# Moving one block of row normalisation out of the first up stage into the attention rounds

## The chip, the cores and the metric

The kernel runs on one core of a Trainium2 chip. The metric is device microseconds of one execution; three executions of the kernel before took 2329.0 to 2330.51, median 2329.72. All times below are microseconds (us) unless marked ns.

TensorE (PE) multiplies, with its weight loads (PEld) shown apart; VectorE (DVE) and ScalarE (ACT) work elementwise; GpSimd (POOL) and SyncE (SP) do little here but issue DMAs. Each engine works through its own queue in order.

## The reference

One transformer block, all in 32-bit floats, on an input of 2 x 2048 x 1024: attention on the normalised rows, then a feed-forward part on the normalised result, both with a residual.

```python
q, k, v = split(layernorm(x) @ Wqkv + bqkv)            # each 2048 x 256
x1 = x + softmax(q @ k.T / 16) @ v @ Wo + bo
z = layernorm(x1)
rw = sum of the two largest of z @ gate_w (8 columns)
f = relu(z @ up_w) ** 2 @ down_w + ((z @ fc1_w) @ expert_w * rw) @ fc2_w
out = x1 + layernorm(f) * ln_gamma + ln_beta
```

## The kernel before, in words

Tokens are handled in eight blocks of 512 rows, each of four row tiles of 128 x 1024. Every product is done three times, with numbers split into a high and a low half (`split`, L140: ScalarE casts the high half, L142, VectorE subtracts to get the low one, L143; `split_late` does the same with the subtraction put off, L149 and L150). The matrix products all stand in `Pass3.add` (L130).

**Projection.** First Q, K and V of all blocks are made (to some 300 us); K and V of the second sequence go to memory and come back later.

**Attention rounds** (L792 on, n = 1 to 8). Round n computes the scores of block n and the product with V of block n - 1, side by side. For each of 16 key chunks k, `scores` makes six matmuls into a PSUM bank of the two-bank pool `psb`; ScalarE copies the bank (L626) and VectorE takes the running maximum (L631); then the bank may be written again. `softmax` subtracts the maximum (L666), takes the exponential on ScalarE (L667), splits the result and adds it to the row sum (L675, L678). At the end `row_max` makes the maximum over all keys (L640), `finish` evacuates the product (L697, L698), and `project` (L707 on) multiplies by Wo: for each of the four row tiles SP loads the residual row (`xres`, L712), GpSimd adds bo to it by an accumulating DMA (L713), VectorE scales each of two banks and adds it to that row (L725), and SP stores the row to `x1` (L728). In rounds 2 to 7 at k = 2 and k = 8 GpSimd also issues a sum of weight quarters between DRAM tensors (`sum_step`, L406 and L408), behind the last bo addition.

**First block of the feed-forward part.** Rounds 2 to 5 load a row tile of `x1[0]` at k = 8 (L818); rounds 3 to 6 normalise it at k = 5 (`norm_row`, L820): BATCH_NORM_STATS on VectorE (L178, L180), the root on ScalarE (L182), the normalisation on VectorE (L203), a transposition in 32 x 32 squares (L213), and a store to a DRAM tile `xt_d` (L218). The last round fetches the four tiles back (`fetch_tile`, L226) and splits them.

**Feed-forward part** (L1142 on). Four passes of 1024 rows (two blocks), each with an up stage and a down stage. A scheme with seven products instead of eight quarters is used, so weights and inputs come in sums of quarters. In the first pass, weight pieces are loaded as `raw` (L903) on SP's queue, cast on ScalarE (L929), split on VectorE (L936), and every other piece is stored for later passes by GpSimd (L939). The second block of the first pass (`x1[1]`) is normalised inside this first up stage: `norm2 = Norm(1)` (L1146), and one `norm2.step()` after each of eleven of the first twelve pieces (L1266). A step loads a row on SP's queue (L1044), makes its statistics, normalises another on ScalarE (L285), transposes and stores a third on GpSimd's queue (L1046), and fetches a fourth. Rows 0 and 2 get their statistics from ScalarE (`Moments`: Identity with a running sum, L261; Square, L273; the root, L274), rows 1 and 3 from VectorE (`Stats`). The fetched tiles are used from the eleventh piece on (L1276). For later passes the same is done in the down stage before.

**What sets the order.** The feed-forward part stands under `tc.manual_schedule()`: each engine gets its instructions in the order of the program. The attention rounds do not: a scheduler orders each engine's queue by the program's priorities and its own estimates of time, and hands out the slots of the tile pools. A row tile (pool `row`, 9 slots of 128 x 1024) holds a residual row, a sum, a loaded Q row, a row to be normalised, or its transposed copy; a load waits until its slot is free, and what stands behind it on SP's queue waits with it.

Of the kernel before, what the change touches and what calls it, by code (L numbers as in the profile page):

```python
# [17 lines left out]
P = 128  # L18
# [7 lines left out]
def kernel(  # L26
# [21 lines left out]
    nc = tc.nc  # L48
# [11 lines left out]
    NB = W // P  # L60
# [20 lines left out]
    def unit(name, dtype=FR):  # L81
        return up.tile([P, U], dtype, tag="u", name=name)
# [4 lines left out]
    def row(name):  # L87
        return rp.tile([P, C], FP, tag="r", name=name)
# [21 lines left out]
    x1 = [dram.tile([W, C], FP, name=f"x1_{i}") for i in range(NBLK)]  # L110
# [29 lines left out]
    def split(t, hi, lo, eng=nc.vector):  # L140

        nc.scalar.copy(hi, t)  # L142
        eng.tensor_tensor(lo, t, f32(hi), ALU.subtract)  # L143
# [46 lines left out]
    def load_row(src, q=nc.sync):  # L190
        r = row("xrow")
        q.dma_start(out=r, in_=src)
        return r

    def norm_row(r, q=nc.gpsimd):
        return norm_write(r, row_stats(r), q)

    def row_stats(r):
        return ln_stats([r[:, ts(h, W)] for h in range(C // W)])
# [5 lines left out]
    def norm_write(r, stats, q=nc.gpsimd):  # L205


        normalise(r, stats)
        return transpose_write(r, q)

    def transpose_write(r, q=nc.gpsimd):
        b = row("xblk")
        nc.vector.transpose(  # L213
            b.rearrange("p (q k i) -> p q k i", q=P // SQ, i=SQ),
            r.rearrange("p (k i q) -> p q k i", k=NCC, i=SQ),
        )
        d = dram.tile([P, C], FP, tag="xt", name="xt_d", bufs=8)
        q.dma_start(out=d, in_=b)  # L218
        return d
# [3 lines left out]
    def fetch_tile(d, q=nc.gpsimd):  # L223

        xt = row("xt")
        fetched[0] = q.dma_start(  # L226
            out=xt.rearrange("p (a f) -> p a f", a=P // SQ),
            in_=d.rearrange("(a i) (q f) -> (i q) a f", i=SQ, q=P // SQ),
        )
        return xt  # L230
# [13 lines left out]
    def split_x(xts, half, t, X, split=split):  # L244
        xv = xts[t].rearrange("p (a k j) -> p k a j", k=NCC, j=SQ)[:, ts(half, NCC // 2)]
        hi, lo = (
            v.rearrange("p (c n) -> p c n", n=W)[:, :, ts(t, P)].rearrange(
                "p c (a j) -> p c a j", j=SQ
            )
            for v in X  # L250
        )
        split(xv, hi, lo)
# [342 lines left out]
    def load_kv(name, src, alloc):  # L595
        t = alloc(name)
        nc.sync.dma_start(out=f32(t), in_=src)
        return t
# [4 lines left out]
    def kv_home(j):  # L603
        return ex_unit if j < 2 * BPB - 1 else unit
# [4 lines left out]
    def start(n, r):  # L609
        st[n] = {"s": [], "p": [], "q": split_q(n, r)}  # L610

    def scores(n, k):
        s = st[n]
        if k % 4 == 0:
            s["s"].append(unit(f"s{n}_{k // 4}", FP))

        wide = n == 0 or n == 1 and k < LAG + 2
        pm = bank(psa if wide and k % 3 else psb, "ps")
        acc = Pass3(pm, NDC)
        kk, q = hl(kv_chunk(n, 0, k)), hl(s["q"])  # L620
        for dc in range(NDC):
            acc.add(
                tuple(kk[:, i, ds(dc * W + (k % 4) * P, P)] for i in range(2)),
                tuple(q[:, i, ts(dc, W)] for i in range(2)),
            )
        nc.scalar.copy(s["s"][k // 4][:, ts(k % 4, W)], pm)  # L626
        if k == 0:
            s["max"] = half(f"max{n}")
            nc.scalar.copy(s["max"], pm)  # L629
        else:  # L630
            nc.vector.tensor_tensor(s["max"], pm, s["max"], ALU.max)  # L631
# [48 lines left out]
    def values(n, k):  # L680
        s = st[n]
        if k == 0:
            s["o"] = [Pass3(bank(psa, "po"), NKC) for _ in range(NDC)]
        v = hl(kv_chunk(n, 1, k))
        for dc in range(NDC):
            s["o"][dc].add(
                tuple(v[:, i, ds((k % 4) * D + dc * P, P)] for i in range(2)),
                tuple(hl(s["p"][k // 2])[:, i, ts(k % 2, W)] for i in range(2)),
            )
# [98 lines left out]

    g_f = half("g_f")[:, : NCC * NE].rearrange("p (c e) -> p c e", c=NCC)
    nc.gpsimd.dma_start(out=g_f, in_=gate_w.rearrange("(c p) e -> p c e", p=P))  # L790
    xts = []
    for n in range(1, NBLK + 1):  # L792
        if n == NBLK:
            X = {p: (unit("xh"), unit("xl")) for p in ("p1", "p2")}

        lag = LAG if n > 1 else LAG + 2
        for k in range(NKC + lag):
            if n + 1 < NBLK:
                if k == 0:
                    q_row = load_row(q_d[n + 1])  # L800
                elif k == NKC // 2:
                    start(n + 1, q_row)
            if n < NBLK and k < NKC:
                scores(n, k)
            if k >= lag:
                values(n - 1, k - lag)
                if n == BPB and (k - LAG) % 4 == 3:
                    j = BPB + (k - LAG) // 4
                    kv[j].append(load_kv(f"v{j}", v_d[j], kv_home(j)))
            if n == 1 and k == 1:  # L810
                softmax(0, 0)
            if n == 1 and k % 2 and 1 < k < NKC:
                softmax(0, k // 2)
            elif n > 1 and k % 2 == 0 and k + 2 < NKC:
                softmax(n - 1, k // 2 + 1)

            if k == NKC // 2 and n in range(2, 2 + NB):
                xts.append(load_row(x1[0][ts(n - 2, P), :]))  # L818
            elif k == 5 and n in range(3, 3 + NB):
                xts[n - 3] = norm_row(xts[n - 3], nc.sync)  # L820
            elif n == NBLK:
                if k < NB:
                    xts[k] = fetch_tile(xts[k], nc.sync)
                elif k % 2 == 0 and k >= 6 and k < 6 + 2 * NB:
                    split_x(xts, 0, k // 2 - 3, X["p1"])
            if k in (2, 8) and 1 < n < NBLK:
                with tc.issue_after(last[0].ins):
                    sum_step(steps.pop(0))
            if n == 1 and k == NKC // 2:
                wo = unit("wo_h"), unit("wo_l")  # L830
                for dc in range(NDC):
                    split(wo_f[dc], *(v[:, ts(dc, C)] for v in wo))
                split(g_f, gate[:, :, 0:NE], gate[:, :, NE : 2 * NE])
            if k == NKC - 1:
                if n == BPB - 1:
                    for j in range(BPB, 2 * BPB):
                        kv[j] = [load_kv(f"k{j}", k_d[j], kv_home(j))]
                if n < NBLK:
                    row_max(n)
        finish(n - 1)  # L840
        if n < NBLK:
            softmax(n, 0)
        project(n - 1)
# [184 lines left out]
    class Norm:  # L1028
# [8 lines left out]
        def step(self, halves=(0, 1)):  # L1037

            load, first, second, norm, write, fetch = (
                self.i - lag for lag in (0, 2, 3, 4, 5, 7)  # L1040
            )
            if 0 in halves:
                if load in range(NB):
                    self.r[load] = load_row(x1[self.n][ts(load, P), :])  # L1044
                if write in range(NB):
                    self.d[write] = transpose_write(self.r[write])  # L1046
                if norm in range(NB):
                    self.m[norm].normalise()
            if 1 in halves:
                if second in range(NB):  # L1050
                    self.m[second].second()
                if first in range(NB):

                    r, by_dve = self.r[first], self.n == 1 and first % 2
                    self.m[first] = Stats(r) if by_dve else Moments(r, "n")
                if fetch in range(NB):
                    self.x[fetch] = fetch_tile(self.d[fetch])
                self.i += 1
# [54 lines left out]
    res_pair, todo, loaded, first, second, written = [], [], [], [], [], []  # L1113
# [28 lines left out]
    t1 = xts  # L1142
    with tc.manual_schedule():
        for b in range(NBB):
            if b == 0:
                norm2 = Norm(1)  # L1146
            x_t = [t1, None]

            h = {}
# [67 lines left out]
            for m, (p, i) in enumerate(UPS[b]):  # L1217
# [45 lines left out]

                if m % 2 and m < 17:
                    out_step()
                if b == 0 and m in (0, 1, 2, 3, 4, 6, 7, 8, 9, 10, 11):  # L1266
                    norm2.step()
                if b == 0 and m < NB:
                    split_x(x_t[0], 1, m, X["p2"], split_late)
                if b == 0 and m % 2 == 0 and 24 <= m < 24 + 4 * NK:  # L1270
# [2 lines left out]

                m4 = 10
                if m == m4:
                    x_t[1] = norm2.x  # L1276
                    X["p4"] = new_x()
                if m > m4 and (m - m4) % 2 and (m - m4) // 2 < NB:
                    split_x(x_t[1], 1, (m - m4) // 2, X["p4"], split_late)
                elif m >= 2 * NK and p != "p7":  # L1280
                    n = {"p4": "p6", "p6": "p5", "p5": "p3", "p3": "p7"}[p]
# [40 lines left out]
            if more:  # L1322
                norm1, norm2 = Norm(2 * b + 2), Norm(2 * b + 3)
            for j, p in enumerate(("p1", "p2", "p6", "p5", "p3", "p7", "p4")):
# [12 lines left out]
                for k in range(NK - late):  # L1337
# [4 lines left out]
                    if more:  # L1342
# [3 lines left out]
                        if j >= 5 and k % 2 and k < 2 * NB:  # L1346
                            n = "p1" if j == 5 else "p2"
# [101 lines left out]
```

## Time and profile before

| what | value |
|---|---|
| three runs, median (lowest to highest) | 2329.72 (2329.0 to 2330.51) us |
| the profiled execution, its own time | 2328.82 us |
| its span in the profile | 2327.1 us |
| granted TensorE clock, mean | 0.998 |
| weight loads busy | 82% |
| bytes moved by DMA | 555.19 MB, mean 239 GB/s |
| HBM read and written | 418.55 and 185.60 MB |

The profile's page lists busy times, the span in 40 slices, the DMA queues, the chain of work that ended last, and the costliest groups of instructions by line. Further views of the same trace give the waits (who waited for whom), the instructions in order of time, DMA issues with the time to their landing, and busy times by stretch. A matmul's end is modelled: a row shows 0.39 us for one, though the next begins 0.23 us later, so a short stall can hide under the shown length, and starts are compared here, not lengths.

### The profile page before, as it was taken

To read this page: it belongs to the slowest core of one execution; us is meant where nothing else is said; L and a number is where in the kernel's file an instruction comes from. 1 tells how busy PE (TensorE), PEld (TensorE's weight loads), DVE (VectorE), ACT (ScalarE), POOL (GpSimd) and SP (SyncE) were. 2 spreads that over 40 slices of the span, in tenths; PEclk is the share of its full clock that TensorE was granted. 3 is DMA by queue.
4 is the path that set the end of the run, shared out by engine and by line. 5 is a ranking of instruction groups with operands and counts; after the bars stand their busy time and mean duration, and the time that the engine had idled before them with its cause. 6 is when DMAs were issued, how large, how long until landed. Compare 5 with 4: busy or idle time off the path is not lost.

```text
span 2327.1 us, 28783 instructions
## 1 busy us (share of the span) xinstructions
PE 2311.7 (99%) x10396; PEld 1898.8 (82%) x10396; DVE 1535.6 (66%) x2315; ACT 1174.4 (50%) x1927; POOL 283.8 (12%) x428
## 2 busy tenths in 40 slices
PE   9999999999999999999999999999999999999998
PEld 7888888888888788888788888878888887888886
DVE  6666569888888575797655577754456675435557
ACT  6555455555543633766552474664055556214235
POOL 3222111011000111110110011110000011000000
PEclk9999999999999999999999999999999999999999
DMA  7878659799977877786887688696568579565684
GB/s 258 301 275 276 240 156 256 232 302 293 228 178 226 269 223 234 241 288 196 251 248 252 219 307 307 189 284 219 194 208 273 193 236 329 188 193 182 204 245 151
DMA packets 226046, 555.19 MB, mean 239 GB/s; under 512 B 18369, under 2 KB 89537, under 8 KB 223857
## 3 DMA queue, kind: packets, MB, share of 16 engines
q1 hardware_dynamic: 158928, 310.43, 40.3%
q0 software_dynamic: 66976, 242.94, 35.5%
q8 instruction: 82, 1.34, 0.2%
q14 instruction: 60, 0.48, 0.1%
HBM read 418.55 MB, written 185.60 MB: 260 GB/s over the span
## 4 chain that ended last, share of the span: by engine, by line
PE 96%; DMA 1%; issue 1%; DVE 1%; ACT 1%; POOL 0%; DVEq 0%; SPq 0%; ACTq 0%; POOLq 0%
PE pd L130 32%; PE pu L130 31%; PE pq L130 7%; PE po L130 7%; PE ps L130 7%; PE pv L446 4%; PE pw L130 4%; PE pg L985 1%; PE pf L130 1%; DMA raw<-in_L_ffn_fc_w_dram 0%; DMA xt<-xt_d 0%; PE psum L701 0%; DVE w L936 0%; DMA w_p<-w 0%; PE pmx L638 0%
## 5 line engine op out<-in xcount | busy, mean ns | idle before, releaser
L130 PE MATMUL pd<-w,sp 128*128 128x512 f32 x3336 | 757.9, 389 | 0.1
L130 PEld LDWEIGHTS pd<-w,sp 128*128 128x128 f32 x3336 | 626.2, 188 | 130.7 <-DVE sp L1192 0.5
L130 PE MATMUL pu<-xh,w 128*128 128x512 f32 x2240 | 693.1, 390 | 1.5 <-DVE w L936 1.4
L130 PEld LDWEIGHTS pu<-xh,w 128*128 128x128 f32 x2240 | 419.3, 188 | 91.2 <-DVE w L936 2.6
L130 PE MATMUL pu<-xl,w 128*128 128x512 f32 x1120 | 436.1, 389 | 0.0
L130 PEld LDWEIGHTS pu<-xl,w 128*128 128x128 f32 x1120 | 210.3, 188 | 44.3 <-DVE xl L150 0.3
L1187 ACT CAST sp<-h 128x512 fp32r<-128x512 f32 x238 | 146.5, 619 | 167.6 <-PE pd L130 130.9
L936 DVE TENSOR_TENSOR w<-w 128x512 fp32r<-128x512 f32 x245 | 167.2, 685 | 80.8 <-ACT w L929 76.9
L929 ACT CAST w<-w 128x512 fp32r<-128x512 f32 x245 | 149.5, 616 | 136.8 <-DMA w<-wt 119.5
L1192 DVE TENSOR_TENSOR sp<-h,sp 128x512 fp32r<-128x512 f32 x238 | 162.5, 685 | 65.6 <-ACT sp L1187 65.4
L130 PE MATMUL po<-p,v 128*128 128x512 f32 x768 | 194.3, 391 | 0.6 <-DVE p L143 0.6
L130 PE MATMUL ps<-q,k 128*128 128x512 f32 x768 | 192.4, 390 | 0.0
L130 PEld LDWEIGHTS ps<-q,k 128*128 128x128 f32 x768 | 143.6, 188 | 30.0 <-ACT max L629 0.2
L130 PEld LDWEIGHTS po<-p,v 128*128 128x128 f32 x768 | 143.0, 188 | 30.2 <-DVE p L143 1.0
L150 DVE TENSOR_TENSOR xl<-xt,xh 128x512 fp32r<-128x512 f32 x108 | 74.3, 688 | 129.8 <-ACT xh L149 129.8
L1137 ACT ACTIVATE h<-h 128x1024 f32<-128x1024 f32 x48 | 50.6, 1055 | 207.5 <-DVE h L1247 158.4
L626 ACT COPY s<-ps 128x512 f32<-128x512 f32 x128 | 74.9, 586 | 135.0 <-PE ps L130 134.9
L213 DVE STREAM_TRANSPOSE xblk<-xrow 128x1024 f32<-128x1024 f32 x60 | 120.8, 2014 | 8.7 <-ACT xrow L285 8.7
L939 POOL DMA_DIRECT2D w_p<-w x105 | 56.1, 535 | 463.6 <-DVE w L936 369.5
L631 DVE TENSOR_TENSOR max<-ps,max 128x512 f32<-128x512 f32 x120 | 82.1, 684 | 33.1 <-ACT s L626 32.1
L130 PE MATMUL pq<-xha,w_h 128*128 128x512 f32 x256 | 99.6, 389 | 0.0
L130 PE MATMUL pq<-xha,w_l 128*128 128x512 f32 x256 | 99.6, 389 | 0.0
(198 smaller groups left out, 2995.4 us busy)
## 6 DMA issues: line engine op xcount, KB each, us to landing
w<-w_p SPq DMA_DIRECT2D x260, 512.0 KB, 3.7
w<-wt SPq DMA_DIRECT2D x235, 256.0 KB, 3.4
w_p<-w POOLq DMA_DIRECT2D x105, 512.0 KB, 4.6
xt_d<-xblk POOLq DMA_DIRECT2D x56, 512.0 KB, 4.1
xt<-xt_d POOLq DMA_DIRECT2D x56, 512.0 KB, 5.7
xres<-in_L_attn_x_dram SPq DMA_DIRECT2D x32, 512.0 KB, 6.9
xres<-in_L_attn_bo_dram POOLq DMA_DIRECT2D x32, 512.0 KB, 10.4
x<-xres SPq DMA_DIRECT2D x32, 512.0 KB, 4.5
```

Source lines behind the costliest of these rows:

```text
L130: nc.tensor.matmul(self.ps, lhsT=a, rhs=b, start=self.i == 0, stop=self.i == self.n - 1, skip_group_check=self.on,)
L150: late_ops.append(lambda: nc.vector.tensor_tensor(lo, t, f32(hi), ALU.subtract))
L213: nc.vector.transpose(b.rearrange("p (q k i) -> p q k i", q=P // SQ, i=SQ), r.rearrange("p (k i q) -> p q k i", k=NCC, i=SQ),)
L446: nc.tensor.matmul(o, lhsT=x_, rhs=w_, start=c + i == 0, stop=c == NCC - 1 and i == 1, skip_group_check=True,)
L626: nc.scalar.copy(s["s"][k // 4][:, ts(k % 4, W)], pm)
L631: nc.vector.tensor_tensor(s["max"], pm, s["max"], ALU.max)
L929: nc.scalar.copy(w[:, 0:W], raw)
L936: nc.vector.tensor_tensor(w[:, W : 2 * W], raw, f32(w)[:, 0:W], ALU.subtract)
L939: nc.gpsimd.dma_start(out=kept[key], in_=w.bitcast(FP))
L1137: nc.scalar.activation(o, v, AF.Relu)
L1187: nc.scalar.copy(t[:, 0:W], v)
L1192: add(t[:, W : 2 * W], v, f32(t)[:, 0:W], ALU.subtract)
```

## The change

The four row tiles of `x1[1]` are loaded, normalised, transposed and stored in rounds 3 to 6, one in each, beside the row of `x1[0]` that is already there: load at k = 6, statistics by ScalarE (`Moments`) at k = 10, normalisation at k = 12, transposition and store (now on SP's queue) at k = 14. The first up stage only fetches the four stored tiles, after pieces 1, 3, 5 and 7. `Norm.step` loses its case for VectorE statistics, which only that block used.

```diff
-    xts = []
+    xts, seconds = [], []
...
             elif k == 5 and n in range(3, 3 + NB):
                 xts[n - 3] = norm_row(xts[n - 3], nc.sync)
+            elif k == 6 and n in range(3, 3 + NB):
+                second_row = load_row(x1[1][ts(n - 3, P), :])
+            elif k == 10 and n in range(3, 3 + NB):
+                second_m = Moments(second_row, "n")
+                second_m.second()
+            elif k == 12 and n in range(3, 3 + NB):
+                second_m.normalise()
+            elif k == 14 and n in range(3, 3 + NB):
+                seconds.append(transpose_write(second_row, nc.sync))
             elif n == NBLK:
...
                 if first in range(NB):
-
-                    r, by_dve = self.r[first], self.n == 1 and first % 2
-                    self.m[first] = Stats(r) if by_dve else Moments(r, "n")
+                    self.m[first] = Moments(self.r[first], "n")
...
         for b in range(NBB):
-            if b == 0:
-                norm2 = Norm(1)
             x_t = [t1, None]
...
-                if b == 0 and m in (0, 1, 2, 3, 4, 6, 7, 8, 9, 10, 11):
-                    norm2.step()
+                if b == 0 and m % 2 and m < 2 * NB:
+                    seconds[m // 2] = fetch_tile(seconds[m // 2])
...
                 m4 = 10
                 if m == m4:
-                    x_t[1] = norm2.x
+                    x_t[1] = norm2.x if b else seconds
```

## The prediction

> **What bounds the kernel now.** I read the first page from the top: busy shares, the chain that ended last, then TensorE's waits.
>
> ```profile
> span 2327.1 us, 28783 instructions
> PE 2311.7 (99%) x10396; PEld 1898.8 (82%) x10396; DVE 1535.6 (66%) x2315; ACT 1174.4 (50%) x1927; POOL 283.8 (12%) x428
> PEclk9999999999999999999999999999999999999999
> PE 96%; DMA 1%; issue 1%; DVE 1%; ACT 1%; POOL 0%; DVEq 0%; SPq 0%; ACTq 0%; POOLq 0%
> ```
>
> TensorE is the bound: 99% busy at full clock, and 96% of the chain. The change neither adds nor removes a matmul, and in the built order of the changed kernel TensorE's rows stand as before, one for one. So only TensorE's stalls can change. All those that the trace names are these (columns: who waited for whom, total, times, longest):
>
> ```profile
> PE busy L513 <- POOL ident masks.py:199: 2.7, 1, 2.7
> PE pu L130 <- DVE w L936: 1.4, 1, 1.4
> PE pt L520 <- DMA ew<-in_L_ffn_expert_w_dram: 0.7, 1, 0.7
> PE po L130 <- DVE p L143: 0.6, 1, 0.6
> ```
>
> The first and third lie in the first 5 us, out of reach. The second is in the first up stage. Next I cut the span into stretches. The columns are the stretch, its length, then busy time and instructions of TensorE, weight loads, VectorE, ScalarE and GpSimd, granted clock, DMA share, GB/s: rounds 3, 4 and 5 (from one output projection to the next), two parts of round 3, the first up stage behind the last projection, the second up stage.
>
> ```profile
> 427.87:484.38 56.51, 56.51 (x258) 46.56 (x257) 49.28 (x60) 30.24 (x40) 6.82 (x8) 1.00 0.84 252
> 484.38:540.82 56.44, 56.44 (x258) 46.58 (x257) 49.22 (x60) 30.21 (x40) 6.78 (x8) 1.00 1.02 307
> 540.82:597.27 56.45, 56.45 (x257) 46.56 (x257) 49.20 (x60) 30.23 (x40) 7.99 (x8) 1.00 1.05 271
> 444.00:466.00 22.00, 22.00 (x98) 18.20 (x97) 21.75 (x26) 13.68 (x18) 3.60 (x5) 1.00 1.00 314
> 466.00:486.00 20.00, 20.00 (x96) 16.34 (x95) 13.38 (x19) 12.16 (x17) 3.22 (x4) 1.00 1.05 269
> 754.99:954.74 199.75, 198.28 (x877) 159.30 (x876) 124.79 (x207) 105.75 (x167) 34.10 (x62) 1.00 0.76 240
> 1145.41:1345.52 200.11, 200.11 (x889) 161.88 (x889) 110.07 (x173) 90.71 (x147) 20.73 (x36) 1.00 0.77 245
> ```
>
> The reader is to see three things. TensorE has no idle time in the rounds, so the place that receives the work can gain nothing. VectorE is 87% busy there, and full from 444 to 466 (21.75 of 22), with slack only in the tail of the round. And the up stage that gives the work away runs little longer than an undisturbed one.
>
> **What the up stage can give back.** TensorE did its first group of 12 matmuls before 754.99. At the steady 0.2267 us each (46 projection matmuls took 10.43 us in the chain) that is 2.72, so the stage cost 199.75 + 2.72 = 202.47 us. The second up stage, with the same matmuls, took 200.11. The excess of 2.4 us is all that can be gained. One stall holds most of it: the last matmul before it starts at 806.02, the next at 807.82, where 806.25 was due, so 1.6 us.
>
> ```profile
> 806.02 0.39 PE L130 MATMUL pu<-xh,w 128*128 128x512 f32 x1
> 807.82 0.50 PE L130 MATMUL pu<-xh,w 128*128 128x512 f32 x1 [1.41 <-DVE w L936]
> ```
>
> The chain of waits behind it: the split at 807.08 stood in VectorE's queue behind the split of a fc1_w piece, whose load was issued only at 794.34 and took 9.30 us; its issue waited for a buffer freed behind work that waited 6.93 us for the fetch of a normalised row, issued at 785.38 after that row's transposition. The change takes out of this stage four transpositions (L213, 4 x 2.02), four BATCH_NORM_STATS (2.6), and some 1.9 us of small instructions, 12.6 us of VectorE; on ScalarE four normalisations (5.0), two Identity and two Square passes (4.4), a table load (1.3), four roots and the small rest (2.4), 13.1 us; four row loads from SP's queue, four row stores from GpSimd's. The four fetches stay but come by the eighth piece, long before use. I take 1.6 for the stall and half of the other 0.8: **-2.0 us**, between 0 (the fc1_w load is late by itself) and -2.4.
>
> **What the rounds must take.** Each of rounds 3 to 6 gets one row. VectorE: one transposition (1.99) and two small instructions (0.16 each), 2.3 us: 49.2 becomes 51.5 of 56.45. ScalarE: Identity and Square passes (1.05 and 1.14, with 0.19 each to read the sum), the mean (0.20), the root (0.30), the normalisation (1.24) and two more table loads (1.28 each), 6.9 us: 30.2 becomes 37.1. TensorE waits in a round if a score bank is still unread: scores k+2 need the maximum k (L631) done. I laid the new order of both queues for round 4 over the durations above and round 3's dates. The new statistics come between scores 4 and 8. ScalarE runs the Square until 452.9, copies scores 7, loads a table, takes the root, copies scores 8 (454.9), loads again (to 456.75), then does the exponential (457.75), a cast (458.75) and the copy of scores 9 (459.3). VectorE then goes: maximum 8 to 456.3, subtraction to 457.45, reciprocal, BATCH_NORM_STATS and product to 458.4, sum to 459.5, a low half to 460.65, maximum 9 to 461.25. TensorE wants that bank for scores 11 at 461.48 (scores begin 1.56 before their copy, here 463.04). Before, maximum 9 ended at 459.4. So 2.0 us of slack become 0.2; at the other maxima 1.4 or more remains. The transposition falls behind maximum 11, at 465.4 to 467.3, in the tail. I take 0.1 a round, **+0.4 us**; bounds 0 (TensorE is saturated: no gain) and 4 x 2.3 = 9.2, if every added VectorE microsecond reached TensorE.
>
> The Trainium skill, "ScalarE: Activation LUTs", section "What ACT_TABLE_LOAD costs", prices a switch of table sets at about 2.66 us, the load and as much again for a drain, and its section on table sets advises to do all of one set before the other, which speaks against this change. The trace shows 1283 ns a load and the next ScalarE instruction 1.28 us after the load began (764.94, then 766.24), so no drain. By the page, an estimate: two switches 2.76 us longer would make maximum 9 late and cost some 2.5 us in each of four rounds, 10 us; by the row, nothing.
>
> **The row slots and SP's queue.** Row tiles share 9 slots, and a round now holds two more. In the built order this moves the residual loads (xres, L712): before, all four are issued early (444.7 to 452.5 in round 3, 500.7 to 502.9 in round 4); now only the first stands ahead of the new row's store on SP's queue, the second behind it, and the third and fourth also behind the loads of K (round 3) or V (round 4), which wait for a buffer. That store waits for the transposition, 467.3 in round 3. GpSimd then adds bo by a DMA of its own (L713), and L725 needs the sum. The wait is not in this trace; these are its rows (KB each, median us to landing, both rounds):
>
> ```profile
> xres<-in_L_attn_bo_dram POOLq DMA_DIRECT2D x8, 512.0 KB, 11.3
> ...
> xres<-in_L_attn_x_dram SPq DMA_DIRECT2D x5, 512.0 KB, 6.5
> ```
>
> Round 3: K's buffer frees near 469.5, so row three is issued at 470.0; with 6.5, 0.9 (GpSimd's issue) and 11.3 it is ready at 488.7, due at 490.77: hidden. Round 4: V's last buffer freed at 529.1, so row three goes out at 529.5 and is ready at 548.2, due at 547.20: 1.0 late. Round 5 has no K or V: row two goes out at 580.5 and is ready at 599.2, due at 600.9. VectorE's next maxima wait behind L725, with 0.4 us of slack there (maximum 1 ended at 440.03, scores 3 began at 440.40), so round 4 loses 0.6: I take **+0.7 us** for all. Ends: nothing, with the shortest rows (5.8 and 8.1), and with the longest of both rounds (12.0 and 17.1) 9 to 12 us in each of rounds 3 and 4. Behind the fourth bo the weight sums (L406, L408) start 14 us later in round 3 and some 29 later in round 4; they took 20 to 42 us to land, and the rounds after have room: nothing.
>
> **Sum.** The profiled run took 2328.82 us (span 2327.1 and 1.7 around it). 2328.82 - 2.0 + 0.4 + 0.7 = 2327.9. The median of three is 2329.72, 0.9 above that run, so on its footing **2328.8 us**. A measurement of this kernel tells about 0.2% (4.7 us) from no change; this is well inside.
>
> **Rivals.**
> Late residual rows (slower): the loads and additions of rounds 3 to 6, four where DMA share is already 0.84 to 1.05, take as long as the slower rows here: 9 (between 6.5 and 12.0), 0.9 and 14.5 (between 11.7 and 17.1), 24.4 us. Then row three is late by 3.6 in round 3 and 6.7 in round 4, row two by 4.0 in round 5, and by some 2 in round 6: 16 us, 2345. It decides where issue to readiness exceeds 17.7 us in round 4 and some 20.5 in rounds 3 and 5. For it: the DMA share, and SP's order. Against: the old 17.1 us came fourth of a burst of four additions (9.7, 11.7, 14.0, 17.1), and the new bursts are of two or three. A loss over 0.2% needs 6.7 us of stalls.
> Full queues: VectorE's 2.3 us reach TensorE in part, say 1 us a round: 2328.8 + 3.6 = 2332.4, still inside 0.2%. For it: the full 444 to 466 stretch. Against: the transposition falls outside it.
> The stall stays: fc1_w's load is late without the rows too; 2328.8 + 2.0 = 2330.8. For it: that load is the slow one (9.30 us). Against: what delayed its issue is gone.
> All gain, no loss: 2329.7 - 2.4 = 2327.3. Faster by more than 0.2% would need more stall than the stage has.
> That nothing moves is excluded by the built order.
>
> **How the numbers follow.** Forecast 0.45, all gain 0.12, stall stays 0.10, full queues 0.14, late rows 0.17, some other gain 0.02. All but the last two lie within 0.2%: 0.81; slower 0.17, faster 0.02. The range goes from the full gain less the spread of the runs (0.7), 2326.5, to 2336, which takes in full queues and the smaller late-row losses.
>
> **What would show it.** Right: no TensorE wait near 806, the first up stage near 200.2 us, rounds 3 to 6 within 1 us of 56.45, L725 waiting for bo at most in round 4. Wrong: L725 waiting for bo by several us in two rounds or more, TensorE waiting for L631 or L725 by over 1 us a round, or a w split still late in the up stage.

## The result, and the profile after

The changed kernel takes **2361.46 us** (median of four runs, 2361.3 to 2362.06) against 2329.54 for the kernel before (four runs, 2329.0 to 2330.51). The ratio is 1.0136, with a 95% interval of 1.0124 to 1.0148: slower by 32 us, where 2328.8 was forecast and 2336.0 was the end of the range. The profiled execution took 2361.49.

The page of the changed kernel, the lines that answer to those of before:

```profile
span 2359.7 us, 28777 instructions
PE 2319.9 (98%) x10396; PEld 1902.3 (81%) x10396; DVE 1531.8 (65%) x2307; ACT 1188.9 (50%) x1945; POOL 281.2 (12%) x424
PE 94%; DMA 3%; DVE 1%; ACT 1%; issue 1%; SPq 0%; DVEq 0%; ACTq 0%
PE pd L130 31%; PE pu L130 31%; PE pq L130 7%; PE po L130 6%; PE ps L130 6%; PE pv L446 4%; PE pw L130 4%; DMA xrow<-x 2%; PE pg L994 1%; PE pf L130 1%; DMA w<-wt 1%; DMA w<-wt_lead 0%; PE psum L701 0%; DVE w L945 0%; DVE sum L675 0%
```

The matmuls are as many as before, but the chain now holds a transfer of its own name: `xrow<-x`, a row load from SP's queue, with 2% of the span. TensorE's waits (who waited for whom, total, times, longest):

```profile
PE ps L130 <- DVE max L631: 24.4, 6, 7.8
PE busy L513 <- POOL ident masks.py:199: 2.7, 1, 2.7
PE pt L520 <- DMA ew<-in_L_ffn_expert_w_dram: 1.3, 1, 1.3
PE po L130 <- DVE p L143: 0.6, 1, 0.6
```

The 1.4 us wait of the up stage is gone. In its place stand six waits for the maximum over a score bank (L631), 24.4 us in all; before there was none. Now the changed kernel by stretches, each round measured from one transposition of its maximum (L638) to the next: rounds 3 to 7, then the first up stage from the same point as before. The columns are the stretch, its length, busy time of TensorE, weight loads, VectorE, ScalarE and GpSimd, granted clock, DMA share, GB/s:

```profile
420.38:477.00 56.62, 56.62 (x257) 46.48 (x257) 51.02 (x62) 36.37 (x49) 1.78 (x2) 1.00 0.55 195
477.00:544.35 67.35, 59.60 (x258) 48.51 (x257) 51.21 (x62) 36.47 (x49) 6.75 (x8) 0.92 0.87 257
544.35:610.81 66.46, 58.48 (x258) 47.43 (x257) 51.03 (x62) 36.41 (x49) 7.63 (x9) 0.95 0.87 262
610.81:670.32 59.51, 57.35 (x258) 46.26 (x257) 49.04 (x57) 33.72 (x46) 7.54 (x8) 1.00 0.96 226
670.32:735.05 64.73, 58.26 (x258) 47.46 (x257) 46.52 (x55) 28.04 (x39) 8.54 (x10) 0.95 0.92 214
788.71:986.63 197.92, 197.84 (x877) 159.41 (x876) 113.16 (x187) 94.77 (x148) 31.17 (x57) 1.00 0.70 220
```

Before, the rounds between the same instructions took 56.47, 56.51, 56.44, 56.45 and 56.54, the up stage 199.75. So the up stage gives back 1.83; round 3 takes its new row for nothing (0.15), and rounds 4, 5, 6 and 7 lose 10.84, 10.02, 3.06 and 8.19. Round 7 has no new row at all. The later stretches and rounds 1 and 2 differ by 0.04 or less, but for the end behind the last matmul (0.7 more, not looked into); what lies ahead of round 1, before anything edited, took 1.45 more (0.04 to 2.75 more in the kernels below).

**Rounds 4 to 6.** Round 4's stall in the instructions in order of time, TensorE first (start, length, instruction, in brackets the idle time before it and who ended it):

```profile
507.38 1.52 PE L130 MATMUL po<-p,v 128*128 128x512 f32 x6
516.65 2.93 PE L130 MATMUL ps<-q,k 128*128 128x512 f32 x6 [7.75 <-DVE max L631]
```

ScalarE in the same view of the changed kernel:

```profile
503.63 1.06 ACT L667 ACTIVATE s<-s 128x1024 f32<-128x1024 f32 x1
514.25 1.06 ACT L261 ACTIVATE junk<-xrow 128x1024 bf16<-128x1024 f32 x1 [9.56 <-DMA xrow<-x]
...
515.31 0.56 ACT L626 COPY s<-ps 128x512 f32<-128x512 f32 x1
```

And VectorE:

```profile
515.90 0.69 DVE L631 TENSOR_TENSOR max<-ps,max 128x512 f32<-128x512 f32 x1 [9.44 <-ACT s L626]
```

Read backwards: TensorE waits for the maximum, VectorE for ScalarE's copy of the scores, and that copy stands in ScalarE's queue behind L261, the Identity pass over the new row, which waits 9.56 us for the row's load. TensorE itself needs nothing of the new row. ScalarE's waits for rows in this kernel (total, times, longest):

```profile
ACT junk L261 <- DMA xrow<-x: 21.6, 3, 9.6
```

The chain of work goes through the load at the same three places (start, length, what):

```profile
498.10 16.13 DMA xrow<-x
...
566.96 15.11 DMA xrow<-x
...
631.84 10.10 DMA xrow<-x
```

Each time the chain runs from the last residual store of the round before, behind which the load is issued, through the whole transfer.

One smaller stall, 1.18 us at 567.17 in round 5, has another cause. VectorE stands at a late residual row there:

```profile
563.98 0.75 DVE L725 SCALAR_TENSOR_TENSOR xres<-pw,ri,xres 128x512 f32<-128x512 f32 x1 [1.74 <-PE ps L130]
```

The view puts the wait down to TensorE, but the matmuls named are scores, which L725 does not read; the fourth bo addition, issued at 555.59, took 8.3 us and landed at 563.89, 0.1 us before L725 began.

**Round 7.** ScalarE, at the next stall of TensorE (6.47 us, ended at 727.78):

```profile
725.78 0.62 ACT L938 CAST w<-w 128x512 fp32r<-128x512 f32 x1 [10.65 <-DMA w<-wt_lead]
726.30 0.58 ACT L626 COPY s<-ps 128x512 f32<-128x512 f32 x1
```

The same pattern with another load: the first piece of weights for the up stage (`wt_lead`), issued at 714.54 and landed in 11.2 us, where before it was issued at 688.98 and took 2.9 to 4.4. Counted from the start of the round both issues stand at 44.2 us, so it is the landing that differs, not the issue.

**Where the slow loads come from.** SP's queue in round 4 of the kernel before:

```profile
496.47 0.38 SPq L192 DMA_DIRECT2D xrow<-x  x1
500.29 0.32 SPq L218 DMA_DIRECT2D xt_d<-xblk  x1
500.70 2.21 SPq L712 DMA_DIRECT2D xres<-in_L_attn_x_dram  x4
507.31 0.33 SPq L597 DMA_DIRECT2D v<-v_d  x1
```

And of the changed kernel (the first `xrow` is the new row, the second that of `x1[0]` for the next round):

```profile
498.10 0.41 SPq L192 DMA_DIRECT2D xrow<-x  x1
501.92 0.32 SPq L218 DMA_DIRECT2D xt_d<-xblk  x1
502.33 0.41 SPq L192 DMA_DIRECT2D xrow<-x  x1
508.93 22.03 SPq L597 DMA_DIRECT2D v<-v_d  x2
531.06 0.38 SPq L712 DMA_DIRECT2D xres<-in_L_attn_x_dram  x1
535.92 0.32 SPq L218 DMA_DIRECT2D xt_d<-xblk  x1
536.30 0.42 SPq L712 DMA_DIRECT2D xres<-in_L_attn_x_dram  x1
```

The four residual loads stood ahead of V; now all stand behind V's first two loads, the second of which holds the queue to 530.9. The bo additions follow the residual loads, and the weight sums (L406, L408), heavy transfers on GpSimd's queue, follow the last bo. Their first issue in rounds 3 to 6: before at 465.81, 510.88, 566.71 and 626.15, after at 487.36, 556.13, 611.44 and 671.56, which is 20, 44, 32 and 23 us later counted from the start of the round. So they now run at the start of the next round, exactly where the new row is loaded behind the four residual stores. The transfers of the 16.1 us of round 4's load, by queue (packets, MB, share of the DMA engines' time; q0 is GpSimd's, q1 SP's):

```profile
q0 software_dynamic: 656, 2.56, 65.4%
q1 hardware_dynamic: 660, 2.43, 39.1%
```

Before, in the 5.6 us of the load at the same place (496.47), q0 had 9 packets and 1.3%.

### The profile page after: what moved, and what is told of

Read it like the earlier page. It is cut to its first block, busy times and chain, and to the rows that moved or that the text cites. A ratio compares the mean times of both kernels' runs of the same rounds, so it can differ in the third digit from the quotient of the medians.

```text
span 2359.7 us, 28777 instructions
## 1 busy us (share of the span) xinstructions
PE 2319.9 (98%) x10396; PEld 1902.3 (81%) x10396; DVE 1531.8 (65%) x2307; ACT 1188.9 (50%) x1945; POOL 281.2 (12%) x424
## 4 chain that ended last, share of the span: by engine, by line
PE 94%; DMA 3%; DVE 1%; ACT 1%; issue 1%; SPq 0%; DVEq 0%; ACTq 0%
PE pd L130 31%; PE pu L130 31%; PE pq L130 7%; PE po L130 6%; PE ps L130 6%; PE pv L446 4%; PE pw L130 4%; DMA xrow<-x 2%; PE pg L994 1%; PE pf L130 1%; DMA w<-wt 1%; DMA w<-wt_lead 0%; PE psum L701 0%; DVE w L945 0%; DVE sum L675 0%
## 5 line engine op out<-in xcount | busy, mean ns | idle before, releaser
L130 PE MATMUL ps<-q,k 128*128 128x512 f32 x768 | 197.7, 398 | 24.4 <-DVE max L631 24.4
L631 DVE TENSOR_TENSOR max<-ps,max 128x512 f32<-128x512 f32 x120 | 82.1, 684 | 49.6 <-ACT s L626 49.0
L130 PE MATMUL pq<-xla,w_h 128*128 128x512 f32 x256 | 99.6, 389 | 0.0
```

The lines of the kernel that those rows point to most:

```text
L130: nc.tensor.matmul(self.ps, lhsT=a, rhs=b, start=self.i == 0, stop=self.i == self.n - 1, skip_group_check=self.on,)
```

## The experiments

The theory after this look: (1) ScalarE stands at L261 for the new row's load in rounds 4 to 6; (2) the load is slow because the weight sums run at its side, and they do because the residual loads moved behind V and the new row's store on SP's queue; (3) the late sums alone make round 7's weight piece late. The rival that was held against it to the end: the added work itself, 2.3 us of VectorE and 6.9 of ScalarE a round, fills the queues. All times below are medians; ratios are to the kernel before, run beside each group on the same chip (medians 2329.8 to 2330.15).

| kernel | median us | ratio (95%) | round 3 | 4 | 5 | 6 | 7 | up stage |
|---|---|---|---|---|---|---|---|---|
| after | 2361.46 | 1.0136 (1.0124 to 1.0148) | 0.15 | 10.84 | 10.02 | 3.06 | 8.19 | -1.83 |
| up_alone | 2328.66 | 0.9996 (0.9987 to 1.0004) | -0.02 | 0.00 | -0.01 | 0.01 | 0.00 | -1.84 |
| no_load | 2344.66 | 1.0063 (1.0051 to 1.0076) | -0.03 | 0.03 | 3.57 | 0.02 | 10.38 | -1.87 |
| pin_stats | 2347.41 | 1.0074 (1.0061 to 1.0087) | -0.03 | 0.89 | 6.70 | -0.01 | 9.36 | -1.80 |
| store_act | 2348.21 | 1.0082 (1.0068 to 1.0096) | 0.16 | 7.66 | 8.25 | 2.11 | 0.02 | -1.84 |
| later_sums | 2343.16 | 1.0056 (1.0043 to 1.0069) | -0.01 | 0.69 | -0.01 | -0.01 | 12.75 | 0.04 |
| pin_store | 2334.75 | 1.0020 (1.0011 to 1.0029) | -0.02 | 0.00 | 7.16 | 0.01 | -0.10 | -1.80 |
| kv_act | 2330.80 | 1.0002 (0.9993 to 1.0011) | 0.59 | 4.85 | -2.63 | -0.02 | -0.54 | -1.84 |
| kv_act_first | 2329.89 | 1.0001 (0.9993 to 1.0010) | 0.60 | 4.87 | -2.58 | 0.63 | -1.49 | -1.83 |
| no_pin | 2336.23 | 1.0025 (1.0015 to 1.0035) | 2.64 | 2.92 | -0.55 | 2.10 | 0.02 | -1.84 |

The columns by round are one profiled execution's time over that of before, worked out as above. In the three kernels with K and V on ScalarE's queue the transposition that marks a round's end moved within the order, so there the sum of rounds 3 to 7 (2.25, 2.03 and 7.13) means more than each. The additions of the residual rows of a round (L725) stand behind that transposition, so a late residual row of round 4 counts in round 5.

**up_alone: the up stage's part by itself.** No second row in the rounds; the up stage fetches the stored tiles of `x1[0]` a second time instead of `x1[1]`'s.

```diff
-            elif k == 6 and n in range(3, 3 + NB):
-                second_row = load_row(x1[1][ts(n - 3, P), :])
...
                 if k < NB:
+                    seconds.append(xts[k])
                     xts[k] = fetch_tile(xts[k], nc.sync)
```

> The up stage's half of the change alone: rounds 3 to 6 get no second row (no load, no statistics, no transposition, no store), and the up stage fetches the four stored tiles of x1[0] a second time in place of x1[1], so the second block's input is left out. My theory that the loss is all in the rounds, and the gain of the up stage is as foreseen (in the changed kernel the stage, from its start to the first down matmul, was 1.8 us shorter than before): 2329.5 - 1.8 = 2327.7 us, and no TensorE wait on L631 in the rounds. Rival, that the up stage without norm steps has its own loss (its weight loads run at other times): 2330 or more.

Measured 2328.66, between the theory's 2327.7 and the rival's 2330, with no wait on L631 in the rounds and the up stage 1.84 shorter. So the gain is real, and as small as forecast: no measurement of whole runs tells it from nothing. All of the loss is in the rounds.

**no_load: the added work without the added load.** The row of `x1[0]` that is there anyway is normalised, transposed and stored a second time.

```diff
             elif k == 5 and n in range(3, 3 + NB):
+                second_row = xts[n - 3]
                 xts[n - 3] = norm_row(xts[n - 3], nc.sync)
-            elif k == 6 and n in range(3, 3 + NB):
-                second_row = load_row(x1[1][ts(n - 3, P), :])
```

> The changed kernel without the load of the new row: the row of x1[0] that was just normalised is normalised, transposed and stored a second time in its place, so the second block's input is left out. All compute and the store stay. Theory A: no instruction of ScalarE waits for a row, so rounds 4 to 6 lose at most 1 us each; the late sums may still hold the lead piece of round 7 (8 us): 2328 to 2340 us. Theory B (the added compute is what the rounds cannot hold): 2350 or more.

Measured 2344.66, above the theory's range and below the rival's. The rounds settle it: with all of the added VectorE and ScalarE work, rounds 3, 4 and 6 cost -0.03, 0.03 and 0.02 over before. The rival falls. What is left lies in round 5 (a stall of 3.2 us) and round 7 (10.38, the weight piece), for the store of the new row still stands on SP's queue ahead of residual loads. In round 5 three of VectorE's additions (L725) wait, 2.05, 0.83 and 1.00 us, and begin at 548.70, 552.09 and 555.63; three bo additions landed at 548.67, 552.02 and 555.57. It also shows the slow landing on a load that both kernels have: the row of `x1[0]` for the next round, issued at 498.5 here, took 18.2 us; in up_alone, issued at 498.2, it took 5.4. GpSimd's queue had 65% of the engines' time in the first case, 1% in the second.

**pin_stats: the statistics later in ScalarE's queue.** They are queued behind the copy of scores 10, by which time the row has landed.

```diff
-        nc.scalar.copy(s["s"][k // 4][:, ts(k % 4, W)], pm)
+        copied[0] = nc.scalar.copy(s["s"][k // 4][:, ts(k % 4, W)], pm)
...
             elif k == 10 and n in range(3, 3 + NB):
-                second_m = Moments(second_row, "n")
-                second_m.second()
+                with tc.issue_after(copied[0].ins):
+                    second_m = Moments(second_row, "n")
+                    second_m.second()
```

> The changed kernel, but the new row's Identity and Square passes are queued on ScalarE behind the copy of scores 10, not behind that of scores 4 as the scheduler had put them in rounds 4 to 6; SP's order, and with it the late residual loads and the late weight sums, stays. Theory A (ScalarE's queue stands at the Identity pass while the row is still on its way, score copies wait behind it, then the maximum, then TensorE): the three waits of rounds 4 to 6 go (they and the slow clock behind them cost 24 us: 10.9, 8.6 and 4.4 by the starts of the projections), the wait for the first lead weight piece in round 7 (8.2 us) stays: some 2338 us. Theory B (the queues of VectorE and ScalarE are too full with the added work, wherever it stands): 2355 or more, with waits of TensorE on L631 still in rounds 4 to 6.

Measured 2347.41: 14 us come back, and ScalarE no longer waits for a row. The row of round 4 landed as late as before (17.7 us); it stood in nobody's way. That is the first link shown by itself. The forecast of the theory was too low because rounds 5 and 7 keep losses of their own: in round 5 TensorE stalls 3.45 us, since L725's additions (here L726) wait for late bo additions (the view names 1.2 us, and two further waits, of 2.75 and 0.51, end within 0.15 us after one landed); in round 7, 7.70 for the weight piece.

**store_act: the new row's store on ScalarE's queue instead of SP's.**

```diff
-                seconds.append(transpose_write(second_row, nc.sync))
+                seconds.append(transpose_write(second_row, nc.scalar))
```

> The changed kernel, but the new row's store is issued from ScalarE's queue, so that the residual loads no longer stand behind it on SP's; ScalarE's Identity pass stays behind the copy of scores 4. Theory A1 (the row's load is late because of the chain: residual loads behind the store, bo additions late, weight sums issued some 20 us late, and these run at the start of the next round beside the row's load, which then takes 10 to 16 us for 5.5): the sums go out near their old places, the load lands in 6 to 8 us, ScalarE's wait falls below 3 us a round and the late lead piece of round 7 goes: 2328 to 2336 us. Theory A2 (the load is late by its place behind four residual stores alone): ScalarE still waits 5 us or more in rounds 4 to 6, 2345 or more.

Measured 2348.21, in the rival's range, but the experiment did not do what it was meant to: V still stood ahead of residual loads, the sums came out at 539.86 and 592.69 in rounds 4 and 5 (27 and 17 us late, counted from the start of the round), the rows took 14.1 and 14.5 us, and ScalarE waited 18.1 us for them. It doesn't separate the two. In round 6 the sums came at 644.43 instead of 671.56, and round 7 lost 0.02 instead of 8.19: a first sign for link 3.

**later_sums: late sums alone, in the kernel before.**

```diff
+            if t == NB - 1 and 0 < n < NBLK - 1:
+                late = small.tile([P, NB], FP, tag="late", name="late")
+                late_at[0] = nc.gpsimd.tensor_tensor(late, r[:, :NB], r[:, :NB], ALU.add)
             nc.sync.dma_start(out=x1[n][ts(t, P), :], in_=r)
...
-                with tc.issue_after(last[0].ins):
+                with tc.issue_after((late_at[0] or last[0]).ins):
                     sum_step(steps.pop(0))
```

> The kernel before, nothing of the change in it; only the weight sums of rounds 3 to 7 queue on GpSimd behind a small addition that reads the last finished residual row, so they are issued some 30 to 45 us later than before, about where the changed kernel issues them. Theory (late sums by themselves make the lead weight piece late): the row load of x1[0] at about 496 lands in 14 to 18 us instead of 5.6, harmless here, and the lead piece stalls TensorE in round 7 by 7 to 10 us: 2336 to 2340. Rival (the sums' date is harmless, the new row's own traffic did it): 2329 to 2331, landings of 5 to 6 us.

Measured 2343.16, 13 us slower than before with nothing of the change in it, and above the 2340 that the theory gave as its end. The first issue of the sums came at 496.94, 553.34, 609.77 and 667.77. TensorE's wait that is new against before:

```profile
PE ps L130 <- DVE max L631: 10.4, 2, 10.0
```

And ScalarE's behind it:

```profile
ACT w L932 <- DMA w<-wt_lead: 14.4, 2, 14.2
```

The four loads of the weight piece were issued from 690.41, 1.4 us later than before, and took 14.7 to 16.9 instead of 2.9 to 4.4: GpSimd's queue had 93.2% of the engines' time meanwhile, before none. Link 3 is shown. The row load at 498.04 took 9.9 us, not the 14 to 18 expected, but nearly twice its 5.6 (the one at 444.93, beside the sums of round 2, 16.8 instead of 5.3); link 2 holds in direction, its size depends on what else is in flight.

**pin_store: the pin and the store together.**

```diff
+                with tc.issue_after(copied[0].ins):
                     second_m = Moments(second_row, "n")
...
+                seconds.append(transpose_write(second_row, nc.scalar))
```

> The change with both single remedies: the statistics of the new row queued on ScalarE behind the copy of scores 10, and the new row's store issued from ScalarE's queue. Theory (three separate losses: ScalarE standing for the landing of the new row, late bo additions in rounds 4 and 5, late weight sums that make the lead weight piece late in round 7): the first is gone by the pin (-13 in its own run), the third by the store (8.19 to 0.02 in its own run), the second at most halved: 2328 to 2332, up stage -1.8. Rival (the losses are one shortage of transfer time that only changes its place): two remedies give no more than one, 2340 or more.

Measured 2334.75, below the rival's 2340 and above the theory's 2332. Singly they give back 14.1 and 13.3, together 26.7, so the rival of one shortage that only changes its place falls. By rounds the two do not add up (in round 4 they give back 9.95 and 3.18 singly, 10.84 together), so that the totals do is in part chance. One stall is left, at 560.48, and it is the residual row that the prediction was concerned with. TensorE's wait:

```profile
PE ps L130 <- DVE max L632: 4.9, 1, 4.9
```

And VectorE's, for the bo addition (the line numbers are one higher here):

```profile
DVE xres L726 <- DMA xres<-in_L_attn_bo_dram: 4.6, 1, 4.6
```

**kv_act and kv_act_first: K and V off SP's queue.** Both add to pin_store that K and V of rounds 3 and 4 are loaded from ScalarE's queue; the second also loads the next row of `x1[0]` at k = 15 instead of 8.

```diff
     def load_kv(name, src, alloc):
         t = alloc(name)
-        nc.sync.dma_start(out=f32(t), in_=src)
+        nc.scalar.dma_start(out=f32(t), in_=src)
```

And in the second alone:

```diff
-            if k == NKC // 2 and n in range(2, 2 + NB):
+            if k == 15 and n in range(2, 2 + NB):
                 xts.append(load_row(x1[0][ts(n - 2, P), :]))
```

> The run with the pin and the store from ScalarE's queue (2334.75), and besides the loads of K and V in rounds 3 and 4 issued from ScalarE's queue, so that on SP's queue no residual load stands behind a load that waits for its buffer. Theory (the one stall left there, 4.9 us at 560.5, is the late third bo addition: its residual load was issued at 531.2, right behind V's two loads that waited until 529.6): the stall goes, 2327.5 to 2330.5, the level of the kernel before less the up stage's 1.8. Rival (the residual loads of round 4 are late because their row slots come free late, whichever queue issues V): 2333 to 2336, the stall stays. Loss from the new place: where a load of K or V waits for its buffer ScalarE waits with it, some us in round 3 or 4.

> As the run before it, and the next row of x1[0] is loaded at the end of the round (k = 15) instead of its middle, so that it holds a row slot for less long. If slots are what makes the residual loads late (the rival there), this one is the faster of the two by 2 to 7 us; if SP's order was (the theory), the two are within 2 us.

Measured 2330.80 and 2329.89, against 2330.03 for the kernel before: no difference that can be told, and within 1 us of each other. The first lies 0.3 above the theory's range, well below the rival's. The residual loads of round 4 go out together at 508.0, the sums at 522.06 and 580.50, and L725 waits for no bo. So SP's order made them late, not the date at which row slots come free. The first kernel's largest waits of TensorE in the rounds:

```profile
PE ps L130 <- DVE max L632: 0.5, 1, 0.5
PE pmx L639 <- DVE max L632: 0.4, 1, 0.4
```

All of the 32 us is accounted for in this way, less some 2 us that rounds 3 to 7 still lose; they eat up the 1.8 of the up stage. What K and V on the other queue would give the kernel before by itself was not tried.

**no_pin: is the pin needed once the sums are early?** As kv_act, without the pin.

```diff
-                with tc.issue_after(copied[0].ins):
-                    second_m = Moments(second_row, "n")
-                    second_m.second()
+                second_m = Moments(second_row, "n")
+                second_m.second()
```

> The run with store, K and V on ScalarE's queue, but without the pin: the new row's statistics stand on ScalarE where the scheduler puts them, early in rounds 4 to 6 (in round 4 behind the copy of scores 1 or 2, about 500 to 505). The weight sums should be issued near their old dates again (463, 522, 580, 633 in the run with the pin), so the new row's load should land in some 7 to 10 us instead of 14 to 17. Theory (the wait of ScalarE is made of the slow landing, and that by the late sums): ScalarE still waits 1 to 5 us in a round, TensorE loses 0 to 3 us in each of rounds 4 to 6: 2331 to 2338. Rival (the place in the queue is enough, whatever the landing): as the run with only the store moved, 2345 or more.

Measured 2336.23, as the theory had it. The new rows of rounds 4, 5 and 6 land in 7.6, 4.2 and 9.9 us, and ScalarE waits for a row in rounds 4 and 6:

```profile
ACT junk L261 <- DMA xrow<-x: 6.8, 2, 3.9
```

That is 2.9 and 3.9 us, where after waited 9.6 and 8.5 in its two longest. So the slow landing made most of the wait. With the place in the queue left as it was, some 5 us remain (2336.23 less 2330.80). That a fast landing would still cost so much is not shown: the larger of the two stalls of TensorE, 2.96 us in round 6, stands behind the load of 9.9 us, during which the sums had 57% of the engines' time; behind the load of 7.6 us (29%) it is 0.82.

## Why the prediction was wrong

**The up stage: right.** Forecast -2.0, measured -1.83, and -1.84 in up_alone. The wait at 806 is gone.

**"I laid the new order of both queues for round 4": the step that failed.** It counted how long each added instruction lasts, and from when its engine is free, but not from when its data is there. The Square "until 452.9" and the Identity before it were placed right behind ScalarE's earlier work, with the row taken as landed; its load, though named in the change, was given no date and no landing time. It is issued behind the four residual stores of the round before, at 498.1 in round 4, and lands 16.1 us later; ScalarE stands 9.56 us for it, and TensorE 7.75 behind ScalarE. On durations alone the step was right: no_load measures 0.03 in round 4 for the added work. The table loads, too, cost what the rows had said: in the changed kernel one begins at 521.06 and the next instruction at 522.36 (1.30 later, as in the prediction's own pair of rows, where it wrote 1.28). "+0.4", with 9.2 as its far end, measured 24.1 in rounds 3 to 6. The far end was wrong as well: a queue that stands behind a load loses the landing, not the length of the added instructions. Round 3, which the dates were taken from, is the one round in which the load met no sums (5.2 and 6.2 us) and nothing was lost.

**"The rounds after have room: nothing": failed too.** The move of the sums was seen, "14 us later in round 3 and some 29 in round 4" (measured 21.6 and 45.3 by date, 20 and 44 from the start of the round). It was asked only when they would be done, not what they would run beside. later_sums prices it: 12.75 in round 7. In rounds 4 to 6 it slows the row loads.

**The residual rows: the mechanism right, the price hidden.** That they would stand behind the new row's store and V was right. In the changed kernel itself L725 waits for bo only once, 1.7 us in round 5, for rounds 4 and 5 are 10 us longer and the due date moves along. Once the first loss is taken away it shows: 7.16 in round 5 of pin_store, where the prediction took 0.7 and its slow rival some 16. Row three, 18.7 us from issue to readiness in the sum, took 22.5 there: its load 14.8 instead of 6.5, the bo addition 7.1 instead of 11.3. The rival's 2345 lay nearer to the result, but by luck: of the changed kernel's 24.4 us of waits its path made 1.2.

**The clock: not in the sum.** The six waits make 24.4 us, but rounds 3 to 7 lose 32.3. Most of the rest is the clock: the matmuls behind the three long stalls began 2.9, 1.5 and 1.5 us later than at full clock. TensorE in round 4 of the changed kernel, in its stall and behind it, by stretches as above, the granted clock third from the end:

```profile
509.00:516.60 7.60, 0.00 (x0) 0.00 (x0) 0.69 (x2) 2.35 (x4) 0.00 (x0) 0.72 1.02 396
516.60:520.00 3.40, 3.35 (x8) 2.67 (x9) 3.40 (x4) 3.37 (x6) 0.00 (x0) 0.50 1.04 418
520.00:524.00 4.00, 4.00 (x14) 3.16 (x13) 3.46 (x4) 2.79 (x6) 0.00 (x0) 0.68 0.66 267
524.00:528.00 4.00, 4.00 (x20) 3.28 (x19) 3.55 (x6) 3.97 (x5) 0.00 (x0) 1.00 0.00 0
```

The three groups of six matmuls after the stall began 2.73, 2.56 and 1.69 us before the next (1.36 at full clock), so 7.75 us of waiting cost 10.65. "TensorE: Matmul & The Clock Gate" of the Trainium skill, section "What's actually happening", has the array's clock fall to half after about 3.4 us without work. The row agrees: 0.50, then full again some 6 us after work began (the third group was slow only at its start). Other stalls here show that their length alone does not decide: after 2.96 us (no_pin, at 621.14), less than the page's figure, the next six matmuls took 2.73 us, and after 3.20 (no_load, at 558.83) only 1.50, at a granted 1.00.

**Skill and landing.** The 656 packets of GpSimd's queue against 660 of SP's in round 4's load are an even share. "DMA: Bandwidth & Descriptors" of the Trainium skill, section "Queues, rings and completion order", says that a DMA engine takes turns between its queues packet by packet; these counts fit it, if the profile's packets fill the page's packets alike in both queues. By that rule alone, as an estimate, a load beside sums of like packets takes about twice as long; it took 5.6 in before, 9.9 in later_sums and 16.1 in after. The times alone do not test it, for SP's queue carried different amounts meanwhile: 489 packets in before, 325 in later_sums, 660 in after. That is 87, 33 and 41 packets per us, so beside the sums SP's queue ran at half its rate or less, and the 16.1 us are that rate and a third more packets. What the further packets were was not taken apart.

## What to carry to other kernels

An instruction that waits for a transfer holds all that stands behind it in its engine's queue: give each added load a date of issue and a landing time beside the traffic that will be there, and place its first reader behind work that the critical engine needs soon. When a change makes one queue's transfers later, ask what those will then run beside, not only when they will be done. A stall of a few us on TensorE can cost more than its length (10.65 for 7.75 here), so price it with the slow matmuls behind it.

## What the runs showed of the hardware

The same row load of 512 KB took 3.8 to 8.1 us where GpSimd's queue had at most 11% of the DMA engines' time, and 9.6 to 20.2 us where its sums had half of it or more. The granted clock fell to about half after stalls of TensorE of 2.96 us (no_pin), 3.45 (pin_stats), 4.91 (pin_store) and 7.75 (here): the next six matmuls took 2.72 or 2.73 us instead of 1.36. It did not fall after 1.18 and 1.72 us here, nor after 3.20 in no_load (1.5 us in each), so no single length divides the two.
